# Layer 1's feed-forward in a decoder on one core: turning rounded rows by DMA, the down product one tile later, and an order by hand for every engine

## The chip, the core and the metric

The kernel runs on one core of a Trainium2 chip. A core has five engines with an instruction queue each: PE (TensorE, matrix products, written into PSUM banks of 128 x 512 float32), DVE (VectorE), ACT (ScalarE), POOL (GpSimd) and SP (SyncE, which here only issues DMAs). Each engine takes its instructions in order; a semaphore wait at the head of a queue holds everything behind it. Transfers between memories are made by the core's 16 DMA engines, whichever queue issued them. The metric is the device time of the program in microseconds (us), as the median of several runs; the profile comes from one execution.

## What is computed

Two decoder layers on 2048 rows (4 batches of 512) of 512 features. Each has self-attention, cross-attention and a feed-forward, each with a residual and a layernorm after it. The change concerns the last of the six: layer 1's feed-forward with rounded weights and rounded activations.

```python
def _quant_weight(w):
    scale = jnp.mean(jnp.abs(w)) + EPS
    return jnp.clip(jnp.round(w / scale), -1.0, 1.0), scale
def _quant_act(x):
    s = jnp.max(jnp.abs(x), axis=-1, keepdims=True) / 127.0 + EPS
    return jnp.clip(jnp.round(x / s), -128.0, 127.0), s
def _qlinear(x, w):
    wq, ws = _quant_weight(w)
    xq, xs = _quant_act(x)
    return jnp.einsum('bsi,oi->bso', xq, wq) * xs * ws
gate = jax.nn.silu(_qlinear(x, w_gate))      # 512 -> 2048
up = _qlinear(x, w_up)                       # 512 -> 2048
return _qlinear(gate * up, w_down)           # 2048 -> 512
...
x = _layernorm(x + _L1_ffn_ref(x, ...), axis=-1)
```

So a row has to be known whole before it can be rounded: once in front of gate and up (512 values), once in front of down (2048 values). The rounded values are whole numbers up to 127, which bfloat16 holds exactly.

## The kernel before

The residual stands in memory as 16 tiles X[t] of 128 rows x 512. Nearly everything before the change's place is the same in both versions: layer 0, layer 1's self-attention, and layer 1's cross-attention. The cross-attention (`l1_xattn`) runs a list of 128 steps and some before and after; a dictionary `todo` holds, for each step, the small pieces of work that `plan` has put there (places EARLY, MIDDLE and LATE of a step), and for PE, DVE and ACT the order in which the program writes instructions there is kept (`tc.manual_schedule`). Among the planned pieces are the rounding of the feed-forward's weights (`quantized`: absolute sums, a scale, the division on DVE (L1064), the clamp on POOL (L1065), the narrowing to bfloat16 on ACT (L1070)), and the layernorm's pieces: `tile_moments` (mean and variance on DVE), `inverse_roots` (the inverse square root on POOL by a first guess and three Newton steps, 15 small instructions) or `table_roots` (the same with ACT's square root and DVE's reciprocal), and `normalise_tile` on DVE.

Then `l1_ffn` follows, a loop over the 16 tiles in which `first(t)` of one tile is written in front of `second(t)` of the tile before (`pipelined`). There is no order by hand: a scheduler places the instructions of each engine.

- `first(t)`: DVE takes the row maximum and makes the scale and its inverse; DVE divides (L1404: multiply by the inverse and add a large constant, which rounds), ACT takes the constant off and narrows to bfloat16 (L1405). `flipped` turns the 128x512 tile with four PE transposes (L1411) and one DVE copy from PSUM (L1412). For each of four quarters n of the 2048 hidden columns PE makes four gate products and four up products (L160, `mm`), ACT applies silu with the row's scale (L1429), and DVE multiplies by the up part (L1430).
- `second(t)`: DVE takes the maximum of each quarter (L1436), makes the scale, divides the four quarters (L1442), ACT narrows each (L1443), `flipped` turns them with 16 PE transposes and four DVE copies; 16 down products follow (L160), and DVE adds them to X[t] (L1450). After every fourth tile comes the layernorm of the batch, with the roots by ACT's table (L243), and four stores by SP (L1454).

PSUM is cut into 3 + 2 + 3 banks (`WIDE`: ps_s for gate, ps_t for transposes, ps_m for up and down).

Of the kernel before, what the change touches and what calls it, by code (L numbers as in the profile page):

```python
# [10 lines left out]
BF16 = mybir.dt.bfloat16  # L11
I32 = mybir.dt.int32
AF = mybir.ActivationFunctionType
# [4 lines left out]
P = 128  # L18
# [68 lines left out]
def decoder_kernel(ctx: ExitStack, tc: tile.TileContext, a: dict, out: bass.AP):  # L87
# [24 lines left out]
    def act(tag, free, bufs=1, dtype=F32):  # L112
        return ap.tile([P, *free], dtype, tag=tag, name=tag, bufs=bufs)

    def tmp(dtype=F32):
        return tp.tile([P, 512], dtype, tag="tmp", name="tmp")

    def small(n, tag, bufs=2):
        return sp.tile([P, n], F32, tag=tag, name=tag, bufs=bufs)

    def prob(tag, free, bufs, dtype=F32):
        return pools["pp"].tile([P, *free], dtype, tag=tag, name=tag, bufs=bufs)

    def pss():
        return pools["ps_s"].tile([P, 512], F32, tag="s", name="ps_s")

    def pst(dtype=F32):
        if "ps_t" not in pools:
            return psm(dtype)
        return pools["ps_t"].tile([P, 512], dtype, tag="t", name="ps_t")  # L130

    def psm(dtype=F32):
        return pools["ps_m"].tile([P, 512], dtype, tag="m", name="ps_m")
# [16 lines left out]
    def tk(t):  # L150
        return slice(t * P, (t + 1) * P)
# [4 lines left out]
    def mm(ps, lhs, rhs):  # L156

        n = len(lhs)
        for i, (x, y) in enumerate(zip(lhs, rhs)):
            PE.matmul(ps, lhsT=x, rhs=y, start=(i == 0), stop=(i == n - 1))  # L160
# [58 lines left out]
        V.bn_stats(st, X[4 * b + i])  # L219
        V.bn_aggr(mv[:, 2 * i:2 * i + 2], st)  # L220

    def inverse_roots(b):


        mv, y = moments[b]
        v, t = small(4, "var"), small(4, "newton")
        G.tensor_scalar(v, mv.rearrange("p (t s) -> p t s", s=2)[:, :, 1], LN_EPS, None, ALU.add)
        G.tensor_scalar(y.bitcast(I32), v.bitcast(I32), -0.5, ROOT_GUESS, ALU.mult, ALU.add)
        G.tensor_scalar(v, v, -0.5, None, ALU.mult)
        for _ in range(3):  # L230
            G.tensor_tensor(t, v, y, ALU.mult)
            G.tensor_tensor(t, t, y, ALU.mult)
            G.tensor_scalar(t, t, 1.5, None, ALU.add)
            G.tensor_tensor(y, y, t, ALU.mult)

    def normalise_tile(b, i):
        mv, rstd = moments[b]
        x = X[4 * b + i]
        V.tensor_scalar(x, x, mv[:, 2 * i:2 * i + 1], rstd[:, i:i + 1], ALU.subtract, ALU.mult)

    def table_roots(b):
        mv, rstd = moments[b]
        A.activation(rstd, mv.rearrange("p (t s) -> p t s", s=2)[:, :, 1], AF.Sqrt, bias=LN_EPS)  # L243
        V.reciprocal(rstd, rstd)

    def layernorm(b):
        for i in range(4):
            tile_moments(b, i)
        table_roots(b)
        for i in range(4):  # L250
            normalise_tile(b, i)
# [63 lines left out]
    def chunks(w):  # L315
        return [w[:, k, :] for k in range(w.shape[1])]
# [764 lines left out]
        plan(scale_at, EARLY, scale_of)  # L1081

# [4 lines left out]
    def l1_xattn():  # L1091
# [183 lines left out]
        def plan(step, place, f, *args):  # L1275
            todo.setdefault((step, place), []).append((f, args))
# [4 lines left out]
        for M in range(4 * B):  # L1281
# [39 lines left out]
                    plan(t0 + x[0], x[1], out_projection, b, i // 2, i % 2, part)  # L1321
            for i in range(4):
                plan(t0 + norms[i], LATE, normalise_tile, b, i)
        for name, n, steps in (("L1_ffn_gateT", INNER, (2, 17, 19)), ("L1_ffn_upT", INNER, (35, 53, 54)),
                               ("L1_ffn_downT", F, (68, 85, 110))):
            quantized(plan, name, n, *steps)
# [66 lines left out]
    def l1_ffn():  # L1393
        wg, sg = quant["L1_ffn_gateT"]
        wu, su = quant["L1_ffn_upT"]
        wd, sd = quant["L1_ffn_downT"]

        def quantize(x, scratch, xq, s):

            V.tensor_reduce(s, x, AX.X, ALU.max, apply_absolute_value=True)  # L1400
            V.tensor_scalar(s, s, 1.0 / 127.0, Q_EPS, ALU.mult, ALU.add)
            inv = small(1, "one", 8)
            V.reciprocal(inv, s)
            V.tensor_scalar(scratch, x, inv, ROUND, ALU.mult, ALU.add)  # L1404
            A.activation(xq, scratch, AF.Copy, bias=-ROUND)  # L1405

        def flipped(dst, src, n):
            for c in range(n // 4):
                pt = pst(BF16)
                for i in range(4):  # L1410
                    PE.transpose(pt[:, tk(i)], src[:, tk(4 * c + i)], identb)  # L1411
                V.tensor_copy(dst[:, 4 * c:4 * c + 4, :], pt.rearrange("p (k n) -> p k n", k=4))  # L1412

        def first(t):
            s = small(1, "one", 8)
            xq, xqt = tmp(BF16), prob("q", [4, P], 3, BF16)
            quantize(X[t], tmp(), xq, s)
            flipped(xqt, xq, 4)
            gs, us = small(1, "one", 8), small(1, "one", 8)
            V.tensor_tensor(gs, s, sg, ALU.mult)  # L1420
            V.tensor_tensor(us, s, su, ALU.mult)
            h = [prob("P", [512], 8) for _ in range(4)]
            for n in range(4):
                pg, pu = pss(), psm()
                nn = slice(512 * n, 512 * n + 512)
                mm(pg, chunks(xqt), [w[:, nn] for w in wg])
                mm(pu, chunks(xqt), [w[:, nn] for w in wu])
                g = tmp()
                A.activation(g, pg, AF.Silu, scale=gs)  # L1429
                V.scalar_tensor_tensor(h[n], pu, us, g, ALU.mult, ALU.mult)  # L1430
            return h

        def second(t, h):
            part, s, inv = small(4, "part4"), small(1, "one", 8), small(1, "one", 8)
            for n in range(4):
                V.tensor_reduce(part[:, n:n + 1], h[n], AX.X, ALU.max, apply_absolute_value=True)  # L1436
            V.tensor_reduce(s, part, AX.X, ALU.max)
            V.tensor_scalar(s, s, 1.0 / 127.0, Q_EPS, ALU.mult, ALU.add)
            V.reciprocal(inv, s)
            hq = prob("v", [4, 512], 1, BF16)  # L1440
            for n in range(4):
                V.tensor_scalar(h[n], h[n], inv, ROUND, ALU.mult, ALU.add)  # L1442
                A.activation(hq[:, n, :], h[n], AF.Copy, bias=-ROUND)  # L1443
            hqt = act("attnT", [16, P], dtype=BF16)
            flipped(hqt, hq.rearrange("p n c -> p (n c)"), 16)
            po = psm()
            mm(po, chunks(hqt), wd)
            ds = small(1, "one", 8)
            V.tensor_tensor(ds, s, sd, ALU.mult)
            V.scalar_tensor_tensor(X[t], po, ds, X[t], ALU.mult, ALU.add)  # L1450
            if t % 4 == 3:
                layernorm(t // 4)
                for i in range(4):
                    nc.sync.dma_start(out[tk(t - 3 + i), :], X[t - 3 + i])  # L1454

        pipelined(range(T // P), first, second)

    l1_ffn()

# [50 lines left out]
```

## Time and profile before

The median of three runs is 2859.72 us (2859.45 to 2869.88).

| | value |
|---|---|
| profiled execution, own time | 2866.8 us |
| its span, first to last instruction | 2865.0 us |
| granted PE clock over the span | 0.984 |
| busy in the span: PE, DVE, ACT, POOL | 2735.0, 1754.2, 1047.2, 422.4 us |
| first gate product of the feed-forward | 2645.8 us |
| first gate product of tile 15 | 2839.05 us |
| last layernorm's normalising ends | 2859.97 us |

A busy row is the sum of the durations of an engine's instructions; the span also holds the idle time. The feed-forward is the last 220 us of the span. In the tables of the profile an entry reads: line of the program, engine, operation, output and input names, shapes and number, then the busy time in us, the mean of one in ns, and the idle time of the engine in front of these instructions with what ended it.

### The profile page before, as it was taken

The page shows a single profiled execution, that of the slowest core. Times are in us where ns is not written, and L with a number is a line of the kernel's source. Part 1 is how long each engine was busy: PE and PEld are TensorE (multiplying, and loading weights), DVE is VectorE, ACT ScalarE, POOL GpSimd, SP SyncE. Part 2 cuts the span into 40 slices and gives each one's busy share as a digit, 9 for nine tenths or more (in the row PEclk, how much of TensorE's full clock was granted, in tenths as well). Part 3 has the DMA queues.
Part 4 walks back from the last instruction along what each step waited for, and adds up shares of the span by engine and source line. Part 5 has one row for each costly group of instructions (what it writes and reads, how often), then busy time and mean ns, then how long its engine had stood idle before and what let it go on. Part 6 is the DMA issues. An engine that isn't in the chain of part 4 may idle for free.

```text
span 2865.0 us, 30441 instructions
## 1 busy us (share of the span) xinstructions
PE 2735.0 (95%) x11434; PEld 1333.5 (47%) x11434; DVE 1754.2 (61%) x3551; ACT 1047.2 (37%) x1929; POOL 422.4 (15%) x436
## 2 busy tenths in 40 slices
PE   7999999998999989999999999999999999999897
PEld 3444444474656445555555554554334334334443
DVE  4565564454121476667766776675766766675998
ACT  2333332233221132233223332233565554554443
POOL 3000000034000401101101110014332322211000
PEclk9999999899999989999999999999999999999999
DMA  9700000003331310000000000111111121010000
GB/s 392 285 15 1 15 4 27 23 21 104 108 119 41 101 57 32 1 1 1 1 0 1 1 1 30 44 59 37 59 59 53 44 74 52 15 52 1 15 16 30
DMA packets 61128, 142.76 MB, mean 50 GB/s; under 512 B 6537, under 2 KB 26010, under 8 KB 54818
## 3 DMA queue, kind: packets, MB, share of 16 engines
q1 hardware_dynamic: 54818, 123.80, 12.2%
q0 software_dynamic: 6144, 16.79, 1.7%
q8 instruction: 99, 1.62, 0.2%
q14 instruction: 67, 0.55, 0.1%
HBM read 84.73 MB, written 47.45 MB: 46 GB/s over the span
## 4 chain that ended last, share of the span: by engine, by line
PE 53%; DVE 10%; POOL 2%; issue 1%; ACT 1%; DMA 0%; POOLq 0%; DVEq 0%; ACTq 0%
PE ps_m L160 16%; PE ps_b L1204 7%; PE ps_m L933 6%; PE ps_s L946 5%; PE ps_m L1215 4%; PE ps_t L963 2%; PE ps_m L978 2%; PE ps_m L1136 2%; PE ps_b L1188 2%; PE ps_m L1261 2%; POOL q L906 1%; DVE P L1430 1%; PE ps_m L1150 1%; PE ps_s L160 1%; DVE tmp L905 1%
## 5 line engine op out<-in xcount | busy, mean ns | idle before, releaser
L1192 DVE TENSOR_REDUCE maxes<-ps_b 128x2 f32<-128x1024 f32 x256 | 312.5, 1223 | 179.1 <-PE ps_b L1188 178.5
L160 PE MATMUL ps_m<-w,attnT 128*128 128x512 f32 (+1 forms) x992 | 384.3, 539 | 0.0
L1208 ACT ACTIVATE PT<-ps_b 128x1024 f32<-128x1024 f32 x256 | 260.7, 1023 | 234.1 <-PE ps_b L1188 152.5
L1188 PE MATMUL ps_b<-k,q 32*128 32x512 f32 x1024 | 286.3, 640 | 1.7 <-ACT PT L1208 1.6
L1204 PE MATMUL ps_b<-q,k 32*128 32x512 f32 x1024 | 283.6, 639 | 0.6 <-ACT PT L1208 0.6
L933 PE MATMUL ps_m<-xT,w 128*128 128x512 f32 x512 | 261.5, 594 | 0.0
L313 DVE TENSOR_TENSOR x<-x,ps_m 128x512 f32<-128x512 f32 x128 | 88.0, 688 | 274.0 <-PE ps_m L160 273.8
L950 ACT ACTIVATE P<-ps_s,nmax 128x512 f32<-128x512 f32 (+3 forms) x256 | 135.2, 528 | 234.8 <-DVE nmax L948 233.6
L160 PEld LDWEIGHTS ps_m<-w,attnT 128*128 128x128 f32 x736 | 138.9, 191 | 162.3 <-issue 159.7
L946 PE MATMUL ps_s<-k,q 128*128 128x512 f32 (+3 forms) x512 | 183.3, 441 | 18.5 <-POOL q L906 16.8
L906 POOL TENSOR_TENSOR q<-tmp 128x512 f32<-128x512 f32 x64 | 81.3, 1270 | 766.2 <-DVE tmp L905 705.1
L978 PE MATMUL ps_m<-PT,v 128*128 128x512 f32 (+3 forms) x512 | 164.0, 444 | 3.0 <-DVE PT L966 3.0
L370 ACT ACTIVATE P<-ps_s,nmax 128x512 f32<-128x512 f32 x128 | 88.4, 692 | 204.5 <-DVE nmax L368 204.4
L957 DVE TENSOR_SCALAR P<-P,sums 128x512 f32<-128x512 f32 (+3 forms) x256 | 151.5, 592 | 5.3
L160 PE MATMUL ps_m<-w,xT 128*128 128x512 f32 (+1 forms) x384 | 143.6, 529 | 4.3 <-DVE v L338 4.3
L1204 PEld LDWEIGHTS ps_b<-q,k 32*128 32x128 f32 x1024 | 75.9, 183 | 147.4 <-issue 119.1
L963 PEld LDWEIGHTS ps_t<-kc,P 128*128 128x128 f32 x640 | 84.0, 141 | 121.3 <-issue 82.0
L978 PEld LDWEIGHTS ps_m<-PT,v 128*128 128x128 f32 x512 | 89.7, 192 | 105.8 <-issue 50.0
L1215 PE MATMUL ps_m<-PT,vv 128*32 128x512 f32 x1024 | 136.4, 605 | 0.6 <-ACT PT L1208 0.6
L348 PE MATMUL ps_m<-xT,w 128*128 128x512 f32 x256 | 122.0, 603 | 9.8 <-DMA w<-in_L_attn_Wq 9.8
L948 DVE TENSOR_REDUCE nmax<-ps_s 128x1 f32<-128x512 f32 (+3 forms) x256 | 125.6, 491 | 5.6
L947 DVE TENSOR_TENSOR ps_s<-ps_s,mask 128x128 f32<-128x128 f32 x256 | 75.3, 294 | 81.0 <-PE ps_s L946 78.9
(281 smaller groups left out, 4405.7 us busy)
## 6 DMA issues: line engine op xcount, KB each, us to landing
hidden<-w SPq DMA_DIRECT2D x16, 1024.0 KB, 16.9
result<-w SPq DMA_DIRECT2D x16, 1024.0 KB, 17.6
w<-in_L_ffn_gateT SPq DMA_DIRECT2D x8, 1024.0 KB, 4.7
tmp<-tmp POOLq DMA_DIRECT2D x64, 128.0 KB, 2.0
w<-in_L_ffn_upT SPq DMA_DIRECT2D x8, 1024.0 KB, 5.1
w<-in_L_ffn_downT SPq DMA_DIRECT2D x8, 1024.0 KB, 5.3
w<-in_L_attn_Wqkv SPq DMA_DIRECT2D x6, 1024.0 KB, 7.1
w<-in_L_attn_Wo SPq DMA_DIRECT2D x5, 1024.0 KB, 11.9
```

Source lines behind the costliest of these rows:

```text
L160: PE.matmul(ps, lhsT=x, rhs=y, start=(i == 0), stop=(i == n - 1))
L933: PE.matmul(ps_q[n], lhsT=wq[h // 4][:, i, tk(h % 4)], rhs=st["xt"][:, i, :], start=(i == 0), stop=(i == 3))
L946: PE.matmul(s[:, :w], lhsT=q[:, tk(qi)], rhs=k[:, :w], start=True, stop=True)
L950: A.activation(p[:, :w], s[:, :w], AF.Exp, bias=nmax[:, qi:qi + 1], accum_out=sums[:, qi:qi + 1])
L957: V.tensor_scalar(p[:, :w], p[:, :w], sums[:, qi:qi + 1], None, ALU.mult)
L963: PE.transpose(pt[:, tk(qi)], probs[qi][:, tk(c)], ident)
L978: PE.matmul(av[:, c * P:], lhsT=st["v"][:, c, tk(g)], rhs=pts[c][:, c * P:], start=(c == 0), stop=(c == 3))
L1188: PE.matmul(s[:, j, :], lhsT=q[strip(i), tk(qi)], rhs=k[strip(i), :], start=True, stop=True)
L1192: V.tensor_reduce(at[:, 2 * half:2 * half + 2, 16 * (1 - g % 2)], s, AX.X, ALU.max, negate=True)
L1204: PE.matmul(s[:, j, :], lhsT=k[strip(i), tk(c)], rhs=q[strip(i), :], start=True, stop=True)
L1208: A.activation(p, s, AF.Exp)
L1215: PE.matmul(avs[g][strip(i), :], lhsT=vv[c][:, 4 * m + i, 16 * par:16 * par + 32], rhs=pts[g, c, i // 2][:, i % 2, :], start=(c == 0), sto ...
```

## The change

- The first two row tiles are rounded and turned inside the cross-attention, as pieces planned for steps 113 to 118 (`first_rows`). They stand in a tile that queries used before ("xT").
- A rounded tile is turned by a DMA from memory to memory that SP issues (`dma_start_transpose`): one of 128x512 for the row (`turn_rounded`), two of 128x1024 for the hidden values (`turn_hidden`). Tile 15's hidden values are still turned by PE, with copies by ACT and DVE.
- The division of the row runs on POOL (`divide`), of the hidden values half on DVE and half on POOL (`divide_hidden`). The hidden values stand in two tiles of 1024 columns, so maxima, divisions and narrowings are taken 1024 wide.
- The down products of tile k-1 follow the gate and up products of tile k on PE; they go to the ps_t banks. The addition to X and the moments of tile k-2 open the next turn.
- The layernorm is taken tile by tile: `inverse_roots` for one column of the batch's statistics, `normalise_tile` and the store on POOL; the last two tiles use ACT's table, DVE and SP.
- The whole loop stands under an order by hand for PE, DVE, ACT, POOL and SP: the order in which the program writes them.

```diff
@@ -219,12 +219,12 @@
         V.bn_stats(st, X[4 * b + i])
         V.bn_aggr(mv[:, 2 * i:2 * i + 2], st)
-    def inverse_roots(b):
-
-
-        mv, y = moments[b]
-        v, t = small(4, "var"), small(4, "newton")
-        G.tensor_scalar(v, mv.rearrange("p (t s) -> p t s", s=2)[:, :, 1], LN_EPS, None, ALU.add)
+    def inverse_roots(b, tiles=slice(0, 4)):
+        mv, y = moments[b][0], moments[b][1][:, tiles]
+        v, t = small(4, "var")[:, tiles], small(4, "newton")[:, tiles]
+        G.tensor_scalar(v, mv.rearrange("p (t s) -> p t s", s=2)[:, tiles, 1], LN_EPS, None, ALU.add)
         G.tensor_scalar(y.bitcast(I32), v.bitcast(I32), -0.5, ROOT_GUESS, ALU.mult, ALU.add)
         G.tensor_scalar(v, v, -0.5, None, ALU.mult)
         for _ in range(3):
@@ -233,14 +233,14 @@
             G.tensor_scalar(t, t, 1.5, None, ALU.add)
             G.tensor_tensor(y, y, t, ALU.mult)
-    def normalise_tile(b, i):
+    def normalise_tile(b, i, engine=V):
         mv, rstd = moments[b]
         x = X[4 * b + i]
-        V.tensor_scalar(x, x, mv[:, 2 * i:2 * i + 1], rstd[:, i:i + 1], ALU.subtract, ALU.mult)
-
-    def table_roots(b):
-        mv, rstd = moments[b]
-        A.activation(rstd, mv.rearrange("p (t s) -> p t s", s=2)[:, :, 1], AF.Sqrt, bias=LN_EPS)
+        engine.tensor_scalar(x, x, mv[:, 2 * i:2 * i + 1], rstd[:, i:i + 1], ALU.subtract, ALU.mult)
+    def table_roots(b, tiles=slice(0, 4)):
+        mv, rstd = moments[b][0], moments[b][1][:, tiles]
+        A.activation(rstd, mv.rearrange("p (t s) -> p t s", s=2)[:, tiles, 1], AF.Sqrt, bias=LN_EPS)
         V.reciprocal(rstd, rstd)
     def layernorm(b):
@@ -1081,6 +1081,31 @@
         plan(scale_at, EARLY, scale_of)
+    rounded = {}
+    def scale_of_row(s):
+        inv = small(1, "one", 8)
+        V.tensor_scalar(s, s, 1.0 / 127.0, Q_EPS, ALU.mult, ALU.add)
+        V.reciprocal(inv, s)
+        return inv
+    def largest(t):
+        s = small(1, "one", 8)
+        V.tensor_reduce(s, X[t], AX.X, ALU.max, apply_absolute_value=True)
+        rounded[t] = s, scale_of_row(s)
+    def divide(t, x):
+        G.tensor_scalar(x, X[t], rounded[t][1], ROUND, ALU.mult, ALU.add)
+    def turn_rounded(t, x, xq, xqt):
+        A.activation(xq, x, AF.Copy, bias=-ROUND)
+        nc.sync.dma_start_transpose(xqt, xq)
+        rounded[t] = rounded[t][0], xqt
@@ -1321,6 +1346,21 @@
                     plan(t0 + x[0], x[1], out_projection, b, i // 2, i % 2, part)
             for i in range(4):
                 plan(t0 + norms[i], LATE, normalise_tile, b, i)
+        def first_rows(t, part):
+            if t == 0 and part == 0:
+                st["rows"] = act("xT", [4, S])
+            x, xq = st["rows"][:, t, :], st["rows"][:, 2 + t, :].bitcast(BF16)
+            if part == 0:
+                largest(t)
+            elif part == 1:
+                divide(t, x)
+            else:
+                turn_rounded(t, x, xq[:, 0:F], xq[:, F:2 * F].rearrange("p (k n) -> p k n", k=4))
+        for t in range(2):
+            for part in range(3):
+                plan(113 + 3 * t + part, LATE, first_rows, t, part)
         for name, n, steps in (("L1_ffn_gateT", INNER, (2, 17, 19)), ("L1_ffn_upT", INNER, (35, 53, 54)),
                                ("L1_ffn_downT", F, (68, 85, 110))):
             quantized(plan, name, n, *steps)
@@ -1395,65 +1435,111 @@
         wu, su = quant["L1_ffn_upT"]
         wd, sd = quant["L1_ffn_downT"]
...
+        both = small(8, "part", 1)[:, 0:2]
+        V.tensor_copy(both[:, 0:1], sg)
+        V.tensor_copy(both[:, 1:2], su)
+        N = T // P
+        hidden, turned, scales, ps_d = {}, {}, {}, {}
+        def scales_of(t):
+            scales[t] = small(4, "sums", 3)[:, 0:2]
+            V.tensor_scalar(scales[t], both, rounded[t][0], None, ALU.mult)
+        def gate_and_up(t, n):
+            if n == 0:
+                hidden[t] = [prob("h", [2, 512], 4) for _ in range(2)], small(4, "nmax", 3)[:, 0:2]
+            pg, pu, g = pss(), psm(), prob("silu", [512], 3)
+            nn, xs = slice(512 * n, 512 * n + 512), chunks(rounded[t][1])
+            mm(pg, xs, [w[:, nn] for w in wg])
+            mm(pu, xs, [w[:, nn] for w in wu])
+            A.activation(g, pg, AF.Silu, scale=scales[t][:, 0:1])
+            V.scalar_tensor_tensor(hidden[t][0][n // 2][:, n % 2, :], pu, scales[t][:, 1:2], g,
+                                   ALU.mult, ALU.mult)
+        def flat(x):
+            return x.rearrange("p k n -> p (k n)")
+        def largest_of(t, i):
+            h, part = hidden[t]
+            V.tensor_reduce(part[:, i:i + 1], flat(h[i]), AX.X, ALU.max, apply_absolute_value=True)
+        def divide_hidden(t):
+            h, part = hidden[t]
+            s, ds = small(1, "one", 8), small(1, "one", 8)
             V.tensor_reduce(s, part, AX.X, ALU.max)
-            V.tensor_scalar(s, s, 1.0 / 127.0, Q_EPS, ALU.mult, ALU.add)
-            V.reciprocal(inv, s)
-            hq = prob("v", [4, 512], 1, BF16)
-            for n in range(4):
-                V.tensor_scalar(h[n], h[n], inv, ROUND, ALU.mult, ALU.add)
-                A.activation(hq[:, n, :], h[n], AF.Copy, bias=-ROUND)
-            hqt = act("attnT", [16, P], dtype=BF16)
-            flipped(hqt, hq.rearrange("p n c -> p (n c)"), 16)
-            po = psm()
-            mm(po, chunks(hqt), wd)
-            ds = small(1, "one", 8)
+            inv = scale_of_row(s)
+            for i, engine in enumerate((V, G)):
+                engine.tensor_scalar(flat(h[i]), flat(h[i]), inv, ROUND, ALU.mult, ALU.add)
             V.tensor_tensor(ds, s, sd, ALU.mult)
-            V.scalar_tensor_tensor(X[t], po, ds, X[t], ALU.mult, ALU.add)
-            if t % 4 == 3:
-                layernorm(t // 4)
-                for i in range(4):
-                    nc.sync.dma_start(out[tk(t - 3 + i), :], X[t - 3 + i])
-
-        pipelined(range(T // P), first, second)
+            hidden[t] = h, ds
+        def turn_hidden(t, i):
+            hq, hqt = prob("hq", [1024], 3, BF16), prob("hqt", [8, P], 4, BF16)
+            A.activation(hq, flat(hidden[t][0][i]), AF.Copy, bias=-ROUND)
+            turned.setdefault(t, []).extend(chunks(hqt))
+            if t < N - 1:
+                nc.sync.dma_start_transpose(hqt, hq)
+                return
+            for c in range(2):
+                pt = psm(BF16)
+                for k in range(4):
+                    PE.transpose(pt[:, tk(k)], hq[:, tk(4 * c + k)], identb)
+                (A.copy, V.tensor_copy)[c](hqt[:, 4 * c:4 * c + 4, :],
+                                           pt.rearrange("p (k n) -> p k n", k=4))
+        def down(t):
+            ps_d[t] = pst()
+            mm(ps_d[t], turned.pop(t), wd)
+        def add_down(t):
+            V.scalar_tensor_tensor(X[t], ps_d.pop(t), hidden.pop(t)[1], X[t], ALU.mult, ALU.add)
+            tile_moments(t // 4, t % 4)
+            (inverse_roots if t < N - 2 else table_roots)(t // 4, slice(t % 4, t % 4 + 1))
+        def store(t):
+            normalise_tile(t // 4, t % 4, G if t < N - 2 else V)
+            (nc.gpsimd if t < N - 2 else nc.sync).dma_start(out[tk(t), :], X[t])
+        for t in range(2):
+            scales_of(t)
+        engines = (nc.tensor, nc.vector, nc.scalar, nc.gpsimd, nc.sync)
+        with tc.manual_schedule(engines={e.engine for e in engines}):
+            for k in range(N + 2):
+                before, behind, ahead = 0 <= k - 1 < N, k >= 2, k + 2 < N
+                if behind:
+                    add_down(k - 2)
+                if before:
+                    turn_hidden(k - 1, 0)
+                if k < N:
+                    gate_and_up(k, 0)
+                if before:
+                    turn_hidden(k - 1, 1)
+                if ahead:
+                    largest(k + 2)
+                    scales_of(k + 2)
+                if k < N:
+                    gate_and_up(k, 1)
+                if behind:
+                    store(k - 2)
+                if k < N:
+                    largest_of(k, 0)
+                if ahead:
+                    x = prob("x", [512], 2)
+                    divide(k + 2, x)
+                if k < N:
+                    gate_and_up(k, 2)
+                if ahead:
+                    turn_rounded(k + 2, x, prob("xq", [512], 2, BF16), prob("xqt", [4, P], 3, BF16))
+                if k < N:
+                    gate_and_up(k, 3)
+                    largest_of(k, 1)
+                    divide_hidden(k)
+                if before:
+                    down(k - 1)
     l1_ffn()
```

## The prediction

> **What bounds the kernel now.** The change touches the last 220 us, so I went from the page to the table of busy times by stretch, each stretch here being one 128-row tile, first matmul of a tile to that of the next. Columns: bounds and length, then busy us of PE, PEld, DVE, ACT and POOL, granted clock, DMA share, GB/s.
>
> ```profile
> 2681.45:2694.36 12.91, 11.97 (x69) 5.79 (x69) 11.83 (x31) 5.68 (x9) 0.00 (x0) 1.00 0.00 0
> 2694.36:2707.27 12.91, 11.96 (x69) 5.82 (x69) 11.88 (x31) 5.67 (x9) 0.00 (x0) 1.00 0.01 2
> 2720.12:2734.01 13.89, 12.02 (x73) 6.08 (x73) 13.82 (x39) 7.36 (x13) 0.00 (x0) 1.00 0.01 2
> ```
>
> PE and DVE are both over 90% full, POOL is empty, and the tile after a layernorm is 1 us longer: 52.56 us for four (2681.45 to 2734.01), 13.14 each. The chain of waits (start, us, engine, line) shows who hands over to whom:
>
> ```profile
> 2685.94 0.88 PE ps_m L160 x4
> 2686.91 0.76 DVE P L1430
> 2692.12 1.19 DVE P L1442 x3
> 2694.36 1.04 PE ps_s L160 x4
> 2695.39 0.86 PE ps_m L160 x4
> ```
>
> The last product of a tile releases DVE; DVE works without a pause; its copy of the turned row releases the next tile. DVE's queue carries the chain, with PE a step behind. Four products start 0.863 us apart (2682.49, 2683.35), so one takes 0.216 us. The durations below come from these groups:
>
> ```profile
> L1430 DVE SCALAR_TENSOR_TENSOR P<-ps_m,one,tmp 128x512 f32<-128x512 f32 x64 | 47.2, 747 | 9.1 <-PE ps_m L160 9.0
> L1411 PE MATMUL ps_t<-identb,v 128*128 128x128 bf16 x256 | 22.3, 219 | 9.0 <-DVE attnT L1412 6.0 <-ACT v L1443 2.9
> L1412 DVE COPY attnT<-ps_t 128x512 bf16<-128x512 bf16 x64 | 24.7, 412 | 0.0
> L1044 DVE TENSOR_REDUCE part<-w 128x1 f32<-128x1024 f32 x24 | 28.9, 1205 | 0.0
> L1064 DVE TENSOR_SCALAR w<-w,wi 128x1024 f32<-128x1024 f32 x24 | 17.6, 732 | 0.0
> L1065 POOL TENSOR_SCALAR w<-w 128x1024 f32<-128x1024 f32 x24 | 24.9, 1037 | 116.8 <-DVE w L1064 92.3 <-PE ps_m L1197 8.8 <-issue 7.8
> L1161 POOL DMA_DIRECT2D tmp<-tmp x64 | 36.0, 564 | 227.8 <-ACT tmp L1142 201.2 <-issue 15.8 <-ACT tmp L1154 10.5
> ```
>
> The number to take from each is the mean of one, in ns, after the busy time. L1044 and L1064 stand earlier in the kernel, in the rounding of the weights, but have the shapes that the new loop uses.
>
> **The engines' sums after.** PE loses the 20 transposes a tile (all but tile 15's) and keeps 48 products: 48 x 0.216 = 10.36 us. DVE loses the five copies (5 x 0.41), half of the division and row rounding; it keeps 4 x 0.747 + 2 reductions of 1024 x 1.205 + the row maximum 0.68 + division 0.73 + add_down 0.75 + moments 0.69 and 0.18 + eight one-column instructions of 0.14 to 0.17: 9.5 us. ACT: 4 x 0.685 (L1429) + 2 x 1.05 (L1070's shape) + 0.63 (L1405) = 5.5 us. Read as sums, PE would be the bound at 10.36, 2.8 us a tile less than now. I don't take that, because of the order on POOL.
>
> **POOL, and the circle it closes.** POOL's queue in a turn of the new loop (its order is fixed by hand) is: its half of the last division, the inverse roots of tile k-2 (15 dependent instructions), normalise k-2, issue the store, divide row k+2. The trace has the same 15 instructions, four columns wide:
>
> ```profile
> 2417.23 0.22 POOL L227 TENSOR_SCALAR var<-mv 128x4 f32<-128x4 f32 x1 [2.10 <-DVE mv L220]
> 2417.53 0.19 POOL L228 TENSOR_SCALAR rstd<-var 128x4 int32<-128x4 int32 x1
> ...
> 2421.29 0.20 POOL L234 TENSOR_TENSOR rstd<-rstd,newton 128x4 f32<-128x4 f32 x1
> ```
>
> 4.26 us, of which width is no part that shows: 0.2 us each and 0.08 between. Behind the wait for tile k-2's moments stand normalise, store and divide k+2; ACT's rounding of row k+2 waits for that divide, and **behind that rounding in ACT's queue stands silu (k, 3)**. DVE needs it for the last quarter of hidden k, then the maximum, the division, and only then add_down k-1 and its moments, which POOL waits for next. So every turn goes once round: 0.10 to POOL + roots 4.26 + normalise 0.63 + store 0.88 + divide 0.55 + rounding on ACT 0.61 + silu 0.69 + quarter on DVE 0.82 + reduction 1.24 + four small ones 0.59 + DVE's half of the division 0.70 + ds 0.07 + add_down and moments 1.69 = **12.83 us a tile**, against 13.14. No buffer loosens it, since each link is an engine's own order. (Links hold the gaps seen in the trace: 0.03 between dependent DVE instructions, 0.1 across engines; overlapping neighbours count 0.07 less.)
>
> Terms that the trace doesn't show:
> - Normalise and divide on POOL with scalars from memory, 128x512. Below: half of L1065's 1.04, 0.52. Above: POOL's two-tensor row of that shape, 1.27 (L906). I take 0.55, for they read one tensor like L1065. The upper end adds 1.4 us a tile.
> - The store's issue, 128 rows: 0.57 (L1161, 64 rows) to 1.01 (L641, indirect, 128 rows). I take 0.80; ends 0.23 either way.
> - Turning by DMA, 128x1024 bf16: nearest row is POOL's memory-to-memory copy of 128 KB, 2.0 us to landing; SP's store of 256 KB takes 2.8. I take 3.0 for 128x1024, 2.4 for 128x512. **A rule speaks against it**: the Trainium skill, "VectorE: DVE Perf Modes", section "The three transpose paths", gives 1309 ns for a 128x128 turn by DMA and 390 for TensorE's. By that price, block after block, a tile's 20 blocks hold the one queue for 26.2 us instead of a tile's 13.14: 15 x 13.06 = 196 us more. TensorE's row here is 0.219. I go by the rows: most of the 2.0 us of a copy is latency, paid once for an instruction of 8 blocks. PE reaches down k-1 about 2.4 us after ACT has rounded the first half, so 3.0 leaves PE waiting 0.7 us, beside the circle; PE has 12.83 - 10.36 = 2.5 us a tile to give, so up to some 5.5 us cost nothing in the running loop, and 7 us some 16 in all.
> - The two halves of the division start together on DVE and POOL. The skill, "SBUF — State Buffer", section "Who interferes with whom", says a two-port tensor_scalar on DVE and a POOL instruction lock each other out. By it POOL's half ends 0.77 + 1.04 = 1.8 us after the maximum; the roots need POOL only at 2.5 (0.70 + 0.07 + 1.69). Hidden either way.
>
> **The other edits.** Rows 0 and 1 are reduced inside cross-attention before as well (two of L1400's 16 stand before 2630); turning them there lifts a 0.86 us gate group into a hole of PE's and the four transposes off the start: first gate counted from 2644.0 instead of 2645.8, -1.8. SP's last load of the down weights now stands behind these two turns, which wait for ACT's rounding of rows that were ready long before: nothing, and were it late, the first that needs these weights is tile 0's down, 16 us into the loop. Of nine table loads of 1.28 us on ACT four stay; the saving is inside the 13.14. The smaller buffers' reuse (silu, h, hq) waits for work a whole tile back. Stores leave SP for POOL, counted.
>
> **The sum.** Before, tile 0's first gate to tile 15's is 193.2 us: 48.5 for the first four tiles, then 11 x 13.15. After: the first turn has no down product (6.9); the second is 13.9, since the first halves come late (DVE starts at 2646.5, as before, with 1.95 us of normalising in it; division 2655, rounded 2657, turned 2660 to 2661) and PE waits 3.5 us; then 10.4 and 11.8 before the circle closes: 43.0. Then 11 x 12.83 = 141.1. Together 184.1: -9.1. Start -1.8. Tail +2.6: from tile 15's first gate to the end 25.95 us before; after, down 14 and then tile 15's own division, rounding, PE transposes, down (3.45), moments, root, normalise (0.54 instead of 1.92) and 5.0 to the end as now: 28.5. Sum -8. The profiled execution took 2866.8 (span 2865.0); the median of the runs is 2859.72, so **2852**.
>
> **Rivals.**
> 1. PE becomes the bound (chance 0.22). For it: the sums, 10.36 against 9.5 and 5.5; against it: POOL's place in ACT's order. If POOL's chain were 2.5 us shorter the circle would open: 11 x 2.47 = 27 to 29 us more, **2823**. Shorter small instructions alone give part of it.
> 2. POOL's two 128x512 instructions at the two-tensor rate (0.15): 12 turns x 1.4, less the 8: +9, **2869**, no change that shows.
> 3. The turns are slow (0.18), the side of slower. Place: SP's single queue and the landing that down k-1 waits for. It decides once a 128x1024 turn holds the queue above 5 us (two and a half of these make 12.8) or lands later than 5.5 us. At 6 us, one after another, a tile takes 6 + 6 + 3.5 = 15.5: 11 x 2.7 = 29, and 18 for the later filling, less the 8: **2899**; by the skill's price 3055.
> 4. The change is one of order only and PE runs as planned: that it does nothing is excluded, since 304 PE transposes leave.
>
> **How the numbers follow.** What a measurement tells from no change is 0.5%, 14 us: 2845.4 to 2874.0. The circle (0.45) is mostly within (0.28); a cheaper store and shorter roots carry it below (0.08), gaps that I haven't counted above (0.09). Rival 1 lies below, 2 within but for 0.01, 3 above. Faster 0.30, same 0.42, slower 0.28. The range reaches to rival 1's end and into rival 3: 2826 to 2882.
>
> **What would show it.** Right: tiles 12.5 to 13.2 us apart, PE waiting 2 us or more a tile, silu (k, 3) behind xq behind POOL's divide, the chain running through POOL's roots. Wrong: turns landing after 6 us, PE waiting for hqt; or tiles at 10.4 with POOL idle before its roots.

## The result, and the profile after

The changed kernel takes **2875.37 us** (median of 13 runs, 2871.71 to 2880.74); the kernel before, run beside it, 2862.65 us (13 runs, 2855.77 to 2869.88). The ratio is 1.0047, 95% interval 1.0037 to 1.0057: 0.5% slower, 13 us, where the forecast was 8 us faster. The time lies in the stated range (2826 to 2882), but on its upper side, which had been widened for slow DMA turns: that it falls inside is luck.

The profiled execution's span is 2871.2 us. Layer 1's cross-attention, ahead of everything that was changed in the loop, began at 1956.0 us in it and at 1963.2 in the profile of before; so both are counted from one fixed point, PE's last group of output products of the cross-attention (2643.42 before, 2635.98 after), to the end of the span:

| stretch, us | before | forecast | after |
|---|---|---|---|
| fixed point to tile 0's first gate product | 2.4 | 0.6 | 1.1 |
| tile 0's gate to tile 4's | 48.5 | 43.0 | 46.6 |
| tile 4's gate to tile 15's (11 tiles) | 144.7 | 141.1 | 159.2 |
| tile 15's gate to the end | 26.0 | 28.5 | 28.3 |
| sum | 221.6 | 213.2 | 235.2 |

(Tile 0's first gate group itself is lifted forward; the place where it would have stood, 0.86 us before its up group, is taken.) Start and tail came nearly as foreseen. The running loop did not: a tile takes 14.48 us, not 12.83.

The table of busy times by stretch, two tiles, with the columns of before's:

```profile
2686.89:2701.37 14.48, 11.48 (x47) 4.75 (x45) 9.12 (x18) 4.94 (x7) 7.99 (x19) 0.88 0.28 63
2715.86:2730.34 14.48, 11.44 (x54) 4.93 (x52) 9.12 (x19) 4.94 (x7) 8.00 (x19) 1.00 0.28 64
```

Now no engine is full: DVE 9.1 of 14.5, POOL 8.0, PE 11.4. In the first of these tiles some of PE's products ran at a lowered clock (0.88 over the tile), in the second none did (1.00), and both take 14.48: the clock doesn't set the period. A loop in which nobody is full and which still has a fixed period points to a circle of waits. The chain of waits over one period (start, us, what):

```profile
2742.85 0.71 POOL x L1100
...
2744.12 0.68 ACT silu L1456
2744.82 0.76 DVE h L1457
2745.61 1.23 DVE nmax L1465
...
2747.51 0.75 DVE h L1473
...
2748.33 0.67 DVE x L1497
...
2750.02 0.23 POOL var L227
...
2754.26 2.10 POOL x L239
2756.35 0.28 issue
2756.65 0.63 POOL out L1503
2757.33 0.71 POOL x L1100
```

The reader should find the same row, POOL's divide (L1100), at both ends, 14.48 us apart, and between them the links that the prediction named, in their order: the rounding on ACT (in the part left out), silu (k, 3), the last quarter, the maximum, the division, add_down, moments, POOL's roots (2750.02 to 2754.26 = 4.24), normalise, store, divide. One length jumps out: 2.10 for normalise (L239). ACT's timeline has the hand-over from POOL to silu:

```profile
2743.58 0.63 ACT L1104 ACTIVATE xq<-x 128x512 bf16<-128x512 f32 x1 [6.04 <-POOL x L1100]
2744.12 0.67 ACT L1456 ACTIVATE silu<-ps_s,sums 128x512 f32<-128x512 f32 x1
```

The groups of instructions say that normalise takes the same in all tiles (the mean of one, in ns, after the busy time):

```profile
L239 POOL TENSOR_SCALAR x<-x,mv,rstd 128x512 f32<-128x512 f32 x14 | 29.3, 2096 | 1.6
L1473 POOL TENSOR_SCALAR h<-h,one 128x1024 f32<-128x1024 f32 x16 | 24.9, 1555 | 60.0 <-DVE one L1090 59.9
L1473 DVE TENSOR_SCALAR h<-h,one 128x1024 f32<-128x1024 f32 x16 | 12.1, 753 | 0.6
L1100 POOL TENSOR_SCALAR x<-x,one 128x512 f32<-128x512 f32 x14 | 10.0, 717 | 27.7 <-DVE one L1090 27.1
L1503 POOL DMA_DIRECT2D out<-x x14 | 9.4, 670 | 7.1 <-POOL x L239 3.9 <-issue 3.2
```

Normalise and divide have the same shape and engine; one takes 2.10, the other 0.72. Of the store's idle time, 3.2 us fall on the first store alone. The list of waits, ten tiles from 2686 to 2830 us (us in total, times, longest):

```profile
ACT xq L1104 <- POOL x L1100: 60.4, 10, 6.0
DVE h L1457 <- ACT silu L1456: 49.2, 10, 4.9
...
PE ps_s L160 <- ACT silu L1456: 26.6, 10, 3.2
PEld L160 <- DMA hqt<-hq: 7.9, 10, 1.3
```

ACT waits 6 us a tile for POOL's divide and DVE 5 us for the silu behind it; the DMA turns hold PE for 0.8 us a tile.

### The profile page after: what moved, and what is told of

The parts are those of the page before. It is cut to its first block, busy times and chain, and to the rows that moved or that the text cites. A ratio compares the mean times of both kernels' runs of the same rounds, so it can differ in the third digit from the quotient of the medians.

```text
span 2871.2 us, 30025 instructions
## 1 busy us (share of the span) xinstructions
PE 2720.1 (95%) x11130; PEld 1315.3 (46%) x11130; DVE 1709.6 (60%) x3347; ACT 1033.6 (36%) x1892; POOL 539.1 (19%) x706
## 3 DMA queue, kind: packets, MB, share of 16 engines
q1 hardware_dynamic: 93186, 130.10, 13.5%
## 4 chain that ended last, share of the span: by engine, by line
PE 51%; DVE 9%; POOL 4%; issue 2%; ACT 2%; POOLq 0%; DVEq 0%; ACTq 0%
PE ps_m L160 14%; PE ps_b L1229 7%; PE ps_m L933 6%; PE ps_s L946 5%; PE ps_m L1240 4%; PE ps_m L978 2%; PE ps_t L963 2%; PE ps_m L1161 2%; PE ps_b L1213 2%; PE ps_m L1286 2%; POOL q L906 1%; PE ps_m L1175 1%; DVE tmp L905 1%; DVE tmp L904 1%; POOL x L239 1%
## 5 line engine op out<-in xcount | busy, mean ns | idle before, releaser
L160 PE MATMUL ps_m<-w,attnT 128*128 128x512 f32 x736 | 325.3, 597 | 0.0
L906 POOL TENSOR_TENSOR q<-tmp 128x512 f32<-128x512 f32 x64 | 81.2, 1269 | 766.4 <-DVE tmp L905 705.2
L160 PE MATMUL ps_m<-w,xT 128*128 128x512 f32 (+2 forms) x416 | 153.1, 521 | 4.7 <-DVE v L338 4.2
## 6 DMA issues: line engine op xcount, KB each, us to landing
w<-in_L_attn_Wo SPq DMA_DIRECT2D x5, 1024.0 KB, 11.8
```

## The experiments

The theory: the circle through POOL's order sets the period, and its normalise is the term that was sized wrongly. Rivals: the DMA turns are late; PE's lowered clock. Left-out code is marked by dots. All kernels are edits of the changed kernel ("changed" below, 2875 us). Each ratio is to the kernel before, run beside it (medians of 2862 to 2865 us).

### 1. The divide ahead of the roots

The link is cut: POOL's divide no longer stands behind roots, normalise and store.

```diff
 def add_down(t):
-            (inverse_roots if t < N - 2 else table_roots)(...)
+            if t >= N - 2:
+                table_roots(...)
 def store(t):
+            if t < N - 2:
+                inverse_roots(...)
...
+                if ahead:
+                    x = prob("x", [512], 2)
+                    divide(k + 2, x)
                 if behind:
                     store(k - 2)
                 if k < N:
                     largest_of(k, 0)
-                if ahead:
-                    x = prob("x", [512], 2)
-                    divide(k + 2, x)
```

> POOL divides row k+2 ahead of the inverse roots, normalise and store of tile k-2, instead of behind them; nothing else moves. Theory (the circle through POOL's order sets 14.48 us a tile): silu (k, 3) no longer stands behind the roots, the circle is open, and what is left is PE with 10.4 us a tile of products or POOL with some 9.6 to 10 us of work, so tiles come 10.4 to 11.5 us apart: 12 x 3 to 4 = 36 to 48 us less than the changed kernel, 2827 to 2840 us, 0.987 to 0.992 of the kernel before. Rival A (the DMA turns' landing holds PE at the down products): PE's wait for hqt comes forward in place of the one for silu, tiles stay above 13 us, at most 20 us less. Rival B (PE runs at a lowered clock for its own sake): no more than 10 us less.

Measured: 2830.21 us, ratio 0.9884 (0.9857 to 0.9911). The same table of busy times, one tile:

```profile
2698.76:2709.12 10.36, 10.31 (x49) 4.70 (x49) 9.21 (x19) 5.16 (x7) 7.59 (x20) 1.00 0.41 92
```

Tiles come 10.36 us apart, PE is full at the full clock, and the DMA turns are the same ones as before. So the circle was the bound, and neither the turns nor the clock was: with the circle, PE's wait and its lowered clock went from the running loop. POOL's rows around the first store show what is left:

```profile
2673.04 2.65 POOL L239 TENSOR_SCALAR x<-x,mv,rstd 128x512 f32<-128x512 f32 x1
2678.92 0.64 POOL L1506 DMA_DIRECT2D out<-x  x1 [3.23 <-issue]
2679.60 1.13 POOL L1473 TENSOR_SCALAR h<-h,one 128x1024 f32<-128x1024 f32 x1
```

POOL stands for 3.23 us in front of its first store, with half of tile 2's division behind it, for which PE's down products then wait.

### 2. The normalise on DVE

```diff
-            normalise_tile(t // 4, t % 4, G if t < N - 2 else V)
+            normalise_tile(t // 4, t % 4)
```

> The normalise of each tile runs on DVE (0.54 us in the profile of before) instead of POOL (2.10 us); roots and store stay on POOL. Theory (the normalise on POOL is the mis-sized term of the circle): a tile loses 2.10 + 0.3 and gains 0.54 + two hand-overs of 0.1, so 14.48 becomes 12.8 to 13.0, 12 x 1.5 to 1.7 = 18 to 20 us less than the changed kernel, some 2856 us, 0.996 to 0.999 of the kernel before; this is what the forecast's circle of 12.83 stood for. Rival A (turns' landing): no change beyond 5 us. Rival B (DVE blocked behind the roots costs what it saves): tiles stay at 14 or more.

Measured: 2861.1 us, ratio 0.9992 (0.9980 to 1.0003); 14 us less than the changed kernel. The chain of waits:

```profile
2735.27 0.56 DVE x L239
2735.83 0.29 issue
2736.12 0.62 POOL out L1503
2736.79 0.71 POOL x L1100
...
2748.04 0.56 DVE x L239
```

The period is 12.77 (2735.27 to 2748.04), where 12.8 to 13.0 was expected, and by it some 19 us should have gone from the fixed point on; 15.9 went (219.3 against 235.2), so that 2861 came of the expected 2856. The trace puts the rest down to the second rival's mechanism in one place: DVE now waits 1.7 us a tile for POOL's roots with its quarters behind it. The running loop still comes out at 12.77 with that wait; at the end it costs time, and from the start of tile 15 to its turning there are 18.2 us instead of 13.5.

### 3. The normalise on POOL in two passes

```diff
-        engine.tensor_scalar(x, x, mv[...], rstd[...], ALU.subtract, ALU.mult)
+        if engine is G:
+            G.tensor_scalar(x, x, mv[...], None, ALU.subtract)
+            G.tensor_scalar(x, x, rstd[...], None, ALU.mult)
...
```

> POOL's normalise is written as two instructions over the 128x512 tile, a subtraction with one scalar from memory and a multiplication with one, in place of one instruction with two. If the second scalar from memory is what makes 2.10 us (the divide with one takes 0.71), two passes take 2 x 0.6 to 0.7 = 1.2 to 1.4 and tiles come at 13.6 to 13.8: 8 to 10 us less than the changed kernel, some 2866 us. If a subtraction or any work in place on X costs this on POOL, each pass takes 1 us or more and the two together 2.1 to 4.2: no gain, up to 25 us more.

Measured: 2889.09 us, ratio 1.0086 (1.0057 to 1.0116), 14 us more. POOL's timeline has 1.58 us for each pass, tiles come 15.5 apart. So it isn't the second scalar alone: a subtraction and a multiplication with one scalar each take over twice the divide's 0.70, which is a multiplication and an addition in one instruction.

### 4. Each turn of hidden values twice

```diff
                 nc.sync.dma_start_transpose(hqt, hq)
+                nc.sync.dma_start_transpose(prob("spare", [8, P], 2, BF16), hq)
```

> Each of the two DMA turns of a tile's hidden values is issued a second time into a spare tile that nothing reads, behind the first on SP's queue: this is work added to what the kernel does. SP then holds 4 x 1.2 + 1.2 = 6 us a tile. Theory (circle through POOL, the turns beside it): tiles stay at 14.48 within 0.1, the time within 3 us of the changed kernel's 2875. Rival A (turns set the tile): the second half's turn lands 1.2 us later or more and so does the down product, 1.2 to 3 us a tile, 18 to 45 us more.

Measured: 2876.68 us, ratio 1.0052 (1.0037 to 1.0067); the period is 14.48 still. Its waits, ten tiles:

```profile
ACT xq L1104 <- POOL x L1100: 60.4, 10, 6.0
...
PEld L160 <- DMA hqt<-hq: 24.1, 20, 2.6
PE ps_s L160 <- ACT silu L1456: 17.2, 9, 2.0
PE ps_t L160 <- DMA hqt<-hq: 13.8, 16, 2.2
```

PE's waits for turned values grew to several times what they were, and its wait for silu shrank in return; the first line, the circle's, did not move by 0.1 us. This is what a cost beside the bound looks like. The landing went from 3.1 to 3.3 us.

### 5. Which form of an instruction POOL serves fast

Nine forms over a spare tile, added in tiles 4 to 9 of the kernel of experiment 1 (r and m: one scalar a row, from memory).

```diff
+    G.tensor_scalar(y, X[t], r, None, ALU.mult)
+    G.tensor_scalar(y, y, r, None, ALU.mult)
+    G.tensor_scalar(y, y, r, 0.0, ALU.mult, ALU.add)
+    G.tensor_scalar(y, y, 1.0, None, ALU.mult)
+    G.tensor_scalar(y, y, 1.0, 0.0, ALU.mult, ALU.add)
+    G.tensor_scalar(y, y, m, r, ALU.subtract, ALU.mult)
+    G.tensor_scalar(y, y, r, m, ALU.mult, ALU.add)
+    G.tensor_scalar(y, y, m, 1.0, ALU.subtract, ALU.mult)
+    G.tensor_scalar(y, y, r, 1.0, ALU.mult, ALU.mult)
```

> The kernel with the divide first, and in tiles 4 to 9 nine more POOL instructions over 128x512 float32 into a spare tile that nothing reads, each in another form; it is run for the durations of these forms, its time has no meaning. So far POOL took 2.10 us for (x - m) * r with both scalars from memory, 1.58 for one operation with one scalar from memory, 0.70 for (x * r) + constant. Theory 1 (each scalar from memory beyond the first costs): only the two forms with two of them lie above 1 us. Theory 2 (subtraction costs): forms with a subtraction are above 1.5, all products and sums near 0.7. Theory 3 (an instruction with a single operation is served slowly): the forms with one operation take about 1.6, with or without a scalar from memory, and (x * r) + 0.0 takes 0.7. Theory 4 (it is X as the operand, or the place of the scalars): reading X is 1.6 and the same form over the spare tile 0.7.

Measured, from the groups of instructions; the nine lines above are L1507 to L1515, and the view sorts by busy time:

```profile
L1512 POOL TENSOR_SCALAR probe<-probe,mv,rstd 128x512 f32<-128x512 f32 x6 | 12.5, 2077 | 0.7
L1514 POOL TENSOR_SCALAR probe<-probe,mv 128x512 f32<-128x512 f32 x6 | 11.9, 1991 | 0.6
L1508 POOL TENSOR_SCALAR probe<-probe,rstd 128x512 f32<-128x512 f32 x6 | 10.4, 1727 | 0.6
...
L1507 POOL TENSOR_SCALAR probe<-x,rstd 128x512 f32<-128x512 f32 x6 | 9.5, 1585 | 0.6
L1510 POOL TENSOR_SCALAR probe<-probe 128x512 f32<-128x512 f32 x6 | 8.9, 1488 | 0.5
...
L1513 POOL TENSOR_SCALAR probe<-probe,rstd,mv 128x512 f32<-128x512 f32 x6 | 4.6, 762 | 0.7
L1509 POOL TENSOR_SCALAR probe<-probe,rstd 128x512 f32<-128x512 f32 x6 | 4.2, 692 | 0.6
L1515 POOL TENSOR_SCALAR probe<-probe,rstd 128x512 f32<-128x512 f32 x6 | 4.1, 687 | 0.6
L1511 POOL TENSOR_SCALAR probe<-probe 128x512 f32<-128x512 f32 x6 | 3.7, 618 | 0.5
```

Theory 3 holds, and of theory 2 that a subtraction costs more; 1 and 4 fall. Two multiplications, or a multiplication and an addition, take 0.62 to 0.76, with no, one or two scalars from memory. One operation alone takes 1.5 to 1.7 (L1507, L1508, L1510), even with a constant. A subtraction as the first of two takes 2.0 to 2.1 (L1512, L1514). Whether X or the spare tile is read makes no such difference (1.59 against 1.73). A subtraction as the second operation was not run. Why POOL serves these forms so differently, no run shows.

### 6. Stores by SP, the divide first

```diff
-            (nc.gpsimd if t < N - 2 else nc.sync).dma_start(out[tk(t), :], X[t])
+            nc.sync.dma_start(out[tk(t), :], X[t])
```

> The kernel with the divide first, and all stores issued by SP in place of POOL. In the divide-first run POOL's first store held its queue 3.22 us, the second half of tile 2's division stood behind it, and PE waited 3.1 us for the turn of that half and then ran some 1.4 us of its products at half rate. If that one store is the price of POOL's queue, 4 to 5 us go: 2825 to 2827 us, 0.986 to 0.988 of the kernel before, and tiles stay at 10.36. Rival (a store that waits on SP for normalise holds up the turns behind it): PE waits for hqt each tile, tiles go to 10.6 or more, 3 us more or worse.

Measured: 2824.89 us, ratio 0.9858 (0.9838 to 0.9878), 5.3 us less than experiment 1; tiles at 10.36. PE's wait at tile 2's down products fell from 3.06 to 1.04 us, and the slowed products behind it are gone. Counted from the fixed point, tile 5's first gate products start at 53.2 us against 56.8 in experiment 1: the traces show 3.7 us for the first store on POOL's queue, where 4 to 5 had been expected.

### 7 and 8. The hidden values turned by PE after all

In the changed kernel (7) and in that of experiment 1 (8): DMA turns of hidden values are replaced by PE's transposes and copies for all tiles, as in tile 15, written behind the second and third quarter.

```diff
                     gate_and_up(k, 1)
+                if before:
+                    turn_late(k - 1, 0)
...
                     gate_and_up(k, 2)
+                if before:
+                    turn_late(k - 1, 1)
```

> The changed kernel, with the hidden values of all tiles turned by PE (16 transposes and four copies a tile, two by ACT and two by DVE) behind the second and the third quarter's products, and no DMA turn of hidden values; rows are still turned by DMA, POOL's order is that of the changed kernel. PE's sum becomes 10.36 + 16 x 0.216 = 13.8 us a tile. Theory (the circle through POOL sets 14.48, PE has room): tiles stay at 14.5, the time is 2875 to 2883 us, the difference being the start. So the change's DMA turns of hidden values gain nothing as long as the circle stands. Rival (the turns' saving is real and something else took it): 12 x 3.5 = 42 us more.

> The same turning by PE in the kernel with the divide first. Theory: with the circle open PE is the bound, and 16 transposes cost their full 3.5 us a tile: tiles at 13.8 to 14.3, 12 x 3.5 to 3.9 = 41 to 47 us more than the divide-first kernel's 2830, so 2871 to 2877 us, 1.003 to 1.006 of the kernel before. Rival (PE was not the bound at 10.36, POOL with its 9.8 us was near enough): less than 30 us more.

Measured: 7 takes 2878.39 us (ratio 1.0052, 1.0031 to 1.0073) at 14.48 a tile: with the circle standing, the DMA turns of the hidden values are worth at most some 3 us in all (2.2 from the fixed point), and the two intervals overlap. 8 takes 2840.28 us (ratio 0.9915, 0.9895 to 0.9934): 10 us more than experiment 1, not 41 to 47. PE's timeline tells why:

```profile
2702.28 1.03 PE L160 MATMUL ps_m<-w,xqt 128*128 128x512 bf16 x4
2703.14 0.61 PE L1490 MATMUL ps_m<-identb,hq 128*128 128x128 bf16 x8
2703.59 1.03 PE L160 MATMUL ps_s<-w,xqt 128*128 128x512 bf16 x3
```

Eight transposes hold the next products up by 0.45 us (2703.14 to 2703.59), 0.056 each. The 0.219 in the group of before is the length of one from start to end, and these overlap; the sum took it for their distance. The timeline of before had it already: eight start at 2688.37, the product behind them at 2688.81. With 16 x 0.056 = 0.9 the period should be 11.26; two tiles' first gate products stand 11.25 apart (2699.69, 2710.94), and 12 x 0.9 = 11 us fit the 10. So PE was the bound in experiment 1, although less than 30 us more had been named as the sign that it wasn't: the expectation failed by a size.

### 9. The normalise on POOL as a product and a sum

```diff
-        engine.tensor_scalar(x, x, mv[...], rstd[...], ALU.subtract, ALU.mult)
...
+        if engine is G:
+            G.tensor_scalar(m, m, r, -1.0, ALU.mult, ALU.mult)
+            G.tensor_scalar(x, x, r, m, ALU.mult, ALU.add)
...
```

> The changed kernel with POOL's order as it is; POOL's normalise is written as x * r + b, with b = -(m * r) from one more 128x1 instruction, the same values by another route. By the durations of the forms (0.76 for a product and a sum with two scalars from memory, some 0.2 at a pitch of 0.28 for the small one) the normalise takes 1.04 in place of 2.10, so tiles come at 14.48 - 1.06 = 13.42 and 12 x 1.06 = 12.7 us go: some 2862 to 2863 us, the kernel before within 0.2%. Rival (in the loop the form is as slow as the subtraction, or the circle has a second branch 0.5 us behind): tiles above 13.8, less than 8 us gained.

Measured: 2864.22 us, ratio 1.0003 (0.9993 to 1.0014), 11 us less than the changed kernel. POOL's timeline:

```profile
2703.33 0.27 POOL L241 TENSOR_SCALAR mv<-mv,rstd 128x1 f32<-128x1 f32 x1
2703.70 0.76 POOL L242 TENSOR_SCALAR x<-x,rstd,mv 128x512 f32<-128x512 f32 x1
2704.76 0.62 POOL L1508 DMA_DIRECT2D out<-x  x1 [0.30 <-POOL x L242]
...
2717.18 0.76 POOL L242 TENSOR_SCALAR x<-x,rstd,mv 128x512 f32<-128x512 f32 x1
```

2703.70 to 2717.18 is 13.48: the period shrank by 1.00, the link by 2.10 - 0.76 - 0.37 = 0.97 (0.37 is the distance from the small instruction's start to the next). No order was changed, only the form of one instruction.

### 10. Stores by SP in the changed kernel

```diff
-            (nc.gpsimd if t < N - 2 else nc.sync).dma_start(out[tk(t), :], X[t])
+            nc.sync.dma_start(out[tk(t), :], X[t])
```

> The changed kernel with all stores issued by SP; POOL's divide then follows normalise at once. Theory (circle): the link 0.30 + 0.63 + 0.05 falls to 0.08 and tiles come at 14.48 - 0.90 = 13.6; with the first store's 3.2 us on POOL gone too, 12 x 0.9 + 3 = 14 us go: some 2861 us, 0.999 to 1.001 of the kernel before. Rival (the store on SP holds the turns behind it and the down products wait): hardly any gain.

Measured: 2860.3 us, ratio 0.9996 (0.9986 to 1.0006), 15 us less than the changed kernel. POOL's timeline:

```profile
2705.22 2.09 POOL L239 TENSOR_SCALAR x<-x,mv,rstd 128x512 f32<-128x512 f32 x1
2707.30 0.69 POOL L1100 TENSOR_SCALAR x<-x,one 128x512 f32<-128x512 f32 x1
...
2718.70 2.10 POOL L239 TENSOR_SCALAR x<-x,mv,rstd 128x512 f32<-128x512 f32 x1
```

The period is 13.48 (2705.22 to 2718.70). 1.00 went: divide now starts as normalise ends, so the whole link of 0.97 is gone, where 0.08 had been left of it in the expectation. The turns on the same queue weren't held up.

### 11. All three

The edits of 1, 6 and 9 together; the last of them:

```diff
+            G.tensor_scalar(x, x, r, m, ALU.mult, ALU.add)
```

> The divide first, all stores by SP, and POOL's normalise as x * r + b. The tiles were at PE's 10.36 already, so 1.06 us less on POOL a tile buys nothing in the running loop; only the first turns, where tile 2's down products waited 1.04 us for a turn behind POOL, can gain: 2822 to 2825 us, 0.985 to 0.987 of the kernel before.

Measured: 2824.14 us, ratio 0.9863 (0.9846 to 0.9879), 10.36 a tile; from the fixed point to the end 183.6 us, against 185.3 without the cheaper normalise (experiment 6). The first turns gained only 0.1 of that (tile 4's first gate products at 42.7 against 42.8 from the fixed point); 1.2 lie behind the start of tile 14's down products, where the granted clock was 0.88 here and 0.82 there. The medians lie 0.75 us apart, less than the spread of either's runs. As expected, the term is worth 1.0 us a tile on the circle and shows nothing beside PE. Experiments 6 and 11 are 1.4% faster than the kernel before and 1.8% faster than the changed one.

## Why the prediction was wrong

- **The bound and its mechanism: right.** The circle that was worked out under "POOL, and the circle it closes" is what the chain after shows, link by link, and experiments 1, 9 and 10 cut or shorten it with the effect that the links' lengths give.
- **The step that failed:** "Normalise and divide on POOL with scalars from memory, 128x512. Below: half of L1065's 1.04, 0.52. Above: POOL's two-tensor row of that shape, 1.27 (L906). I take 0.55, for they read one tensor like L1065." Normalise measured 2.10, outside both ends; divide 0.71. The two were taken as one kind because they read one tensor each. What counts is the form: divide is a multiplication and an addition (fast, experiment 5), normalise begins with a subtraction (slow). L1065, a minimum and a maximum, could not bound it. The Trainium skill, "GPSIMD Engine Reference", section "3.1 Elementwise — side-by-side cycle accounting", has 768 ns as the best case of a tight loop over 512 elements; here the fast forms lie at or under it (0.62 to 0.76), and normalise takes 2.7 times as long.
- **The sum with the measured term:** normalise +1.47 (2.10 and its gaps for 0.63), store +0.09 (0.97 for 0.88), divide +0.16 (0.71 for 0.55), all else -0.07: 12.83 + 1.65 = 14.48. Eleven tiles make 18.1 us. The four first tiles took 3.6 us more than the sum: the fourth took 16.4 for 11.8, by the first store's wait of 3.2 on POOL and the normalise's 1.5, and the second 12.9 for 13.9. The sum has no term for that wait. The L1161 row that the prediction shows has 15.8 us of "issue" in front of POOL's DMAs, and the timeline of before has two such waits, 5.76 in front of the first of them and 10.01 in front of a later one; whether they are of the same kind, no run shows. 18.1 + 3.6 + 0.5 at the start - 0.2 in the tail = 22.0 between the forecast 213.2 and 235.2.
- **The rival of POOL's rate** pointed the right way (it gave 2869) and had the wrong limit: two-tensor reads at 1.27.
- **PE as the bound:** not in the changed kernel, but exactly this once the circle is open: 10.36 a tile, 2830 where 2823 was said (2825 once the first store's wait is off POOL).
- **The DMA turns:** 3.1 us to landing for 128x1024 (3.0 taken), 2.4 for 128x512 (2.4 taken), 1.2 us of SP's queue each; experiment 4 shows the room beside the circle. By the 1309 ns that the Trainium skill ("VectorE: DVE Perf Modes", section "The three transpose paths") gives for a 128x128 turn, paid block after block, eight would take 10.5 us, an estimate; an instruction of eight blocks took 3.1. TensorE's side was also mis-sized, 0.219 for 0.056 a block, which did no harm to the forecast since PE's 10.36 counts the 48 products alone.
- **The two halves of the division:** POOL's takes 1.60 when it starts 0.13 us behind DVE's 0.75, and 1.13 when it runs apart from it (experiment 1). That agrees in kind with the lock in the rule that was weighed: they overlap for 0.62 us, and 0.47 are added. As foreseen it lay off the circle.
- **Start and tail:** 1.1 for 0.6 and 28.3 for 28.5.

## What to carry to other kernels

When an order by hand puts a slow engine's long work in front of a short piece that another engine waits for, add the links round the loop before adding up engines: here nobody was over 80% full in the mean of the tiles, and moving one 0.7 us instruction ahead of 7.3 us of other work gave 45 us. The duration of an instruction is borrowed only from a row with the same operations, not just the same engine, shape and number of inputs; where no such row exists, widen the bound. For a short instruction that overlaps with its neighbours, take the distance between starts, not the mean length.

## What the runs showed of the hardware

- On POOL the same 128x512 float32 tile costs 0.62 to 0.76 us as `x*a*b` or `x*a + b`, 1.5 to 1.7 us with one operation, 2.0 to 2.1 us as `(x-a)*b`. Writing the last as `x*b + (-a*b)` took it to 0.76, with 0.37 more for the scalar.
- POOL's first store in this loop waits 3.2 us in front of its issue, in every kernel here whose stores and normalise POOL takes, the later ones 0.3 (3.8 and 0.9 in experiment 2, where they also wait for DVE). The cause is open; issued by SP, the stores show no such wait.
- After a wait of 2 to 3 us in each tile PE ran part of its products at half rate in some of the tiles: of eight tiles in a row from 2686.89 in the changed kernel, four have a granted clock of 0.88 and four of 1.00. With the circle open the clock of a tile in the running loop is 1.00. PE's timeline after the change:

```profile
2745.80 1.03 PE L160 MATMUL ps_m<-w,xqt 128*128 128x512 bf16 x4
2749.98 1.06 PE L160 MATMUL ps_s<-w,xqt 128*128 128x512 bf16 x4 [3.16 <-ACT silu L1456]
2750.84 1.91 PE L160 MATMUL ps_m<-w,xqt 128*128 128x512 bf16 x4
```

In this tile the first group after the wait is still fast, and the second takes 1.91 for 1.03. The wait's length alone doesn't decide it: one tile earlier, after a wait of 3.07 us (2735.49), both groups took 1.03, and two tiles after that, after a wait of only 2.21 (2764.46), both were slow. It cost nothing here: tiles with and without it take 14.48.
